# The query product on 64-by-64 parts of TensorE's array, in two passes between scores and values

## The chip, the cores and the metric

The kernel runs on one core of one Trainium2 chip. The metric is the device time of one execution in microseconds; the time of a kernel is the median of its runs. Before the change it is 2009.44 us, the median of three runs from 2009.4 to 2009.89 us. A second number is the span of one profiled execution, from its first to its last recorded instruction, which all rows of the profile refer to.

## The reference

One transformer layer in float32 on x of shape (32, 512, 256): a windowed attention with 16 query heads and 4 key/value heads, then a feed-forward product with a gated sum of eight low-rank terms.

```python
x = x + attn(_layernorm(x), wq, wk, wv, wo, q_norm_w, k_norm_w)
x = x + ffn(_layernorm(x), weight, gate_w, lora_U, lora_V)

def attn(x, ...):                      # DIM, H, KV, HD, WIN = 256, 16, 4, 64, 128
    q = rmsnorm((x @ wq.T).reshape(B, T, H, HD), q_norm_w)
    k = rmsnorm((x @ wk.T).reshape(B, T, KV, HD), k_norm_w)
    v = (x @ wv.T).reshape(B, T, KV, HD)
    k, v = jnp.repeat(k, 4, axis=2), jnp.repeat(v, 4, axis=2)
    scores = jnp.einsum('bqhd,bkhd->bhqk', q, k) / jnp.sqrt(HD)
    mask = (i >= j) & (i - j < WIN)
    a = jax.nn.softmax(jnp.where(mask, scores, -jnp.inf), axis=-1)
    return jnp.einsum('bhqk,bkhd->bqhd', a, v).reshape(B, T, H * HD) @ wo.T

def ffn(x, ...):                       # E, R = 8, 16
    gate = jax.nn.softmax(x @ gate_w.T)
    t = jnp.einsum('nh,erh->ner', x, lora_U)
    return x @ weight.T + jnp.einsum('ne,eor,ner->no', gate, lora_V, t) / R
```

## The kernel before

The 32 sequences of 512 tokens are cut into 128 tiles of 128 tokens, so four tiles make a sequence; tile t = 0 of a sequence has no tile before it. All tiles go through the same steps, and the kernel is a software pipeline over them: the function `slot(i)` (L805) lists one period, in which each step works on a tile that is some number of tiles behind i. The order in which every engine gets its instructions is written out by hand: `slot` for the middle, and two tables, FIRST and LAST, for the tiles at either end. There is no scheduler behind it; each engine's instructions stand in the order of these calls, and an engine whose next instruction has to wait holds back all that stands behind it.

The steps on TensorE, per tile, with the lines of the profile:

- `q_pe(gp)` (L418): the query product, in two halves of 512 columns (eight heads each), called with gp = 1 and gp = 0 at two places of a period. The stationary operand is xT, the transposed tile (two chunks of 128 features by 128 tokens), the moving one wq_sb. Each half is two matmuls on the full 128-by-128 array into one bank of PSUM, q0 or q1.
- `kv_pe` (L403): keys and values in one product of the same size.
- `s_pe(j)` (L535): scores of block j of 32 queries, j = 3, 2, 1, 0, eight matmuls on 64-by-64 parts of the array with up to 160 columns; four of them fill the array, two row halves by two column halves.
- `y_pe` and `yb_pe` (both L624): values, again on 64-by-64 parts with 256 columns. In `y_pe` the upper row half writes bank y0 and the lower one y1; in `yb_pe` rows and banks are exchanged. Between them stands `y_mark` (L653), a copy of one column of y1 on ScalarE (ACT) which `yb_pe` waits for, so that the two row halves never write one bank at one time. Tiles with t = 0 have no mixed part (`vd` and `other`) in `y_pe`.
- `o_pe` (L673), the output projection on the full array; `ug_pe` and `base_pe` (L720) and `lora_pe` (L775), the feed-forward products, full array, banks g and f.

In float32 the trace counts two records on TensorE for each matmul that is called.

ACT empties the banks: `q_copy` (L426) and `qsq` (L431) read each q bank, `kv_copy` and `ksq` (L409, L413) the kv bank, `y_copy` (L667) the y banks; `exps` (L562) reads the scores after DVE (VectorE) has merged the window's edges and taken the maxima (`s_merge` L546, `nmaxs` L551). POOL (GpSimd) raises the variances to the power -1/2 (`rsqrt`, L329), scales q and k (`qn` L463, `kn` L454) and the probabilities (`prob` L574), and masks (`pick` L605). DVE transposes by 32-by-32 blocks into a buffer of pieces; `move(n)` (L363) sends them in 16 DMAs on SP's queue to their places, from where ACT (kT, hT, uT) and TensorE (scores and values) read them.

PSUM has four single banks, B0 to B3, and two double ones, S0 and S1, for the scores. The table BANK says which products take turns in which bank in the middle of the kernel, and PLACES the exceptions of the tiles at the ends. A product waits until the last reader of the bank's former product is done.

In the middle of the kernel the order on TensorE was o(i-10), lora(i-16), q1(i-2), s2 and s3(i-5), y(i-8), q0(i-2), kv(i-2), yb(i-8), s1 and s0(i-5), g(i-12), f(i-15).

Of the kernel before, what the change touches and what calls it, by code (L numbers as in the profile page):

```python
# [8 lines left out]
F32 = mybir.dt.float32  # L9
# [5 lines left out]
P = 128  # L15
# [4 lines left out]
ND = D // P  # L20
# [10 lines left out]
def tile_window_attn_lora_ffn(  # L31
# [45 lines left out]
    nc = tc.nc  # L77
    B, T, _ = x.shape
    NT = T // P
    N = B * NT  # L80
    GP = KV // 2
# [29 lines left out]
    for tag, products in {  # L111
        "B0": "tk uT q1 kv",
        "B1": "ckv cqa cqb y0 o",
        "B2": "cf tq0 tq1 f y1",
        "B3": "hT q0 g",
        "S0": "s2 s0",
        "S1": "s3 s1",
    }.items():
        BANK.update(dict.fromkeys(products.split(), tag))
# [3 lines left out]
        ("ckv", 0): "B3",  # L123
        ("cqb", 0): "B2",
        ("kv", 0): "B3",
        ("cqa", 0): "B0",
        ("q1", 0): "B1",
        ("q0", 0): "B0",
        ("q1", 1): "B3",
        ("q0", 1): "B1",  # L130
        ("tk", 0): "B1",
        ("kv", 2): "B2",
        ("tq1", 0): "B3",
        ("q0", 2): "B1",
        ("tq0", 1): "B1",
        ("tq1", 1): "B3",
        ("tk", 1): "B3",
        ("q0", 3): "B2",
        ("kv", 3): "B2",
        ("tq0", 2): "B3",  # L140
        ("tq1", 2): "B3",
        ("q0", 4): "B1",
        ("q1", 4): "B2",
        ("kv", 4): "B3",
        ("q1", 5): "B2",
        ("q1", 6): "B3",
        ("y0", 0): "B2",
        ("y1", 0): "B1",
        ("q0", 6): "B0",
        ("kv", 6): "B1",  # L150
        ("y0", 2): "B2",
        ("y1", 2): "B1",
        ("o", 2): "B3",
        ("y0", 4): "B3",
        ("y1", 4): "B1",
        ("g", 0): "B2",
        ("o", 4): "B2",
        ("o", 5): "B2",
        ("g", 3): "B2",
        ("f", 0): "B1",  # L160
        ("o", 6): "B3",
        ("q0", -2): "B1",
        ("y0", -8): "B3",
        ("y1", -8): "B0",
        ("kv", -2): "B2",
        ("q0", -1): "B1",
        ("y0", -7): "B0",
        ("kv", -1): "B1",
        ("o", -8): "B2",
        ("y0", -6): "B3",  # L170
        ("y1", -6): "B0",
        ("y1", -5): "B0",
        ("o", -6): "B2",
        ("g", -8): "B0",
        ("y0", -4): "B3",
        ("y1", -4): "B0",
        ("o", -4): "B2",
        ("uT", -7): "B3",
        ("y1", -3): "B0",
        ("hT", -4): "B1",  # L180
        ("o", -3): "B0",
        ("y1", -2): "B3",
        ("o", -2): "B0",
        ("g", -6): "B0",
        ("f", -8): "B1",
        ("g", -5): "B2",
        ("uT", -6): "B2",
        ("y0", -1): "B3",
        ("y1", -1): "B0",
        ("g", -4): "B2",  # L190
        ("uT", -5): "B1",
        ("hT", -3): "B1",
        ("g", -3): "B1",
        ("uT", -4): "B1",
        ("o", -1): "B0",
        ("hT", -1): "B1",
        ("f", -5): "B1",
        ("g", -1): "B0",
        ("uT", -2): "B3",
        ("f", -4): "B3",  # L200
        ("f", -2): "B3",
# [166 lines left out]
    class Tile:  # L368
# [45 lines left out]

        def q_pe(self, gp):
            ps = self.bank(f"q{gp}")
            for c in range(ND):
                nc.tensor.matmul(  # L418
                    ps, self.xT[:, c, :], wq_sb[:, c, gp * 512 : (gp + 1) * 512],
                    start=(c == 0), stop=(c == ND - 1),  # L420
                )

# [228 lines left out]
        def y_mark(self):  # L651
            mark = small.tile([P, 1], F32, tag="mark", name=f"mark_{self.n}")
            nc.scalar.copy(mark, self.ps["y1"][:, :1])  # L653
# [151 lines left out]
    def slot(i):  # L805
        at(i - 4).trk()
        at(i - 6).exps(0)
        at(i - 12).hT_copy()
        at(i - 10).o_pe()
        at(i - 13).ln2_rs()  # L810
        at(i - 16).lora_pe()
        move(i - 7)
        at(i - 13).gmax()
        at(i - 16).store()
        at(i - 16).put()
        at(i - 2).q_pe(1)
        at(i - 5).kT_copy()
        at(i - 6).exps(1)
        at(i - 8).pick(1)
        at(i - 6).tr(2)  # L820
        at(i - 13).gexp()
        at(i - 10).o_add()
        at(i - 13).gmul()
        at(i - 2).qsq(1)
        at(i - 3).q_eps()
        at(i - 5).s_pe(2)
        at(i - 6).prob_den(0)
        at(i - 2).q_copy(1)
        at(i - 8).pick(0)
        at(i - 5).s_pe(3)  # L830
        at(i).ln1_stats()
        at(i - 8).y_pe()
        at(i - 5).s_merge(3)
        at(i - 5).nmaxs(3)
        at(i - 2).q_pe(0)
        at(i - 15).uT_copy()
        at(i - 5).s_merge(2)
        at(i - 2).kv_pe()
        at(i - 8).y_mark()
        at(i - 5).exps(3)  # L840
        at(i - 10).trh()
        at(i - 8).yb_pe()
        at(i - 2).q_copy(0)
        at(i - 1).trx()
        at(i - 6).prob(0)
        at(i - 5).nmaxs(2)
        at(i - 5).s_pe(1)
        at(i - 5).exps(2)
        at(i - 11).ln2_stats()
        at(i - 2).qsq(0)  # L850
        at(i - 5).s_pe(0)
        at(i - 1).ln1_rs()
        at(i - 3).pow()
        at(i - 3).kn()
        at(i - 6).vdiff()
        at(i - 6).tr(1)
        at(i - 13).tru()
        at(i - 3).qn()
        at(i - 6).tr(0)
        at(i - 12).ln2_eps()  # L860
        at(i - 6).tr(3)
        at(i - 8).y_copy(1)
        at(i - 5).s_merge(1)
        at(i - 5).prob_den(1)
        at(i - 12).ug_pe()
        at(i - 8).y_copy(0)
        at(i).ln1_eps()
        at(i - 5).nmaxs(1)
        at(i - 2).kv_copy()
        at(i - 2).ksq()  # L870
        at(i - 5).s_merge(0)
        at(i - 5).prob(1)
        at(i - 5).nmaxs(0)
        at(i - 3).trq()
        at(i - 2).ksum()
        at(i - 15).base_pe()
        at(i - 2).qsum()
        load_x(i + 1)
        load_blocks(i + 3)
# [3 lines left out]
        ldb:0 ldb:1 ldx:0 ldb:2 mean_kv:0 ldb:3 sub_kv:0 mean_qb:0 ln1_stats:0 trx:0 sub_qb:0 ldx:2  # L883
        mean_qa:0 ln1_eps:0 ldb:5 sub_qa:0 kv_pe:0 q_pe.1:0 q_pe.0:0 ln1_rs:0 ldx:1 kv_copy:0 ksq:0
        ln1_stats:2 trx:1 q_copy.1:0 qsq.1:0 ln1_stats:1 q_pe.0:1 ldx:5 ldx:4 ln1_eps:2 ln1_rs:2
        ldwv:0 ksum:0 ln1_stats:4 ln1_eps:1 qsq.0:0 ln1_rs:1 ldx:6 ln1_eps:4 ln1_rs:4 trx:3 qsum:0
        q_copy.0:0 q_eps:0 kv_pe:1 trx:2 ldx:8 kv_copy:1 q_pe.1:1 qsq.0:1 qsq.1:1 ksq:1 ksum:1 ldx:3
        q_copy.0:1 kv_pe:2 pow:0 q_pe.1:2 q_copy.1:1 qsum:1 kv_copy:2 q_eps:1 ksq:2 kn:0 tk_pe:0
        qn:0 tq_pe.1:0 ldx:9 kT_copy:0 ldb:4 tq_pe.0:0 ldb:6 ldx:7 qsq.1:2 ln1_stats:7 ldx:11 pow:1
        tq_copy.1:0 ksum:2 q_pe.0:2 tq_copy.0:0 ln1_stats:6 ln1_stats:3 s_pe.3:0 qsq.0:2 q_copy.0:2  # L890
        s_pe.2:0 ln1_eps:3 s_merge.3:0 nmaxs.3:0 qsum:2 s_merge.2:0 q_copy.1:2 kn:1 nmaxs.2:0
        kv_pe:3 ln1_stats:5 tk_pe:1 qn:1 exps.3:0 q_eps:2 q_pe.1:3 ldb:7 kT_copy:1 ln1_rs:3 ldb:10
        vdiff:2 kv_copy:3 pow:2 s_pe.1:0 exps.2:0 ldx:10 s_merge.1:0 ksq:3 trx:4 tq_pe.1:1 kn:2
        nmaxs.1:0 tq_pe.0:1 ksum:3 s_pe.0:0 s_merge.0:0 nmaxs.0:0 ln1_stats:8 q_pe.0:3 qsq.1:3
        tq_copy.1:1 prob_den.1:0 kv_pe:4 tq_copy.0:1 exps.1:0 qsq.0:3 qn:2 vdiff:3 exps.0:0 s_pe.3:1
        q_pe.0:4 s_pe.2:1 ldx:12 qsum:3 prob_den.0:0 q_copy.1:3 ln1_stats:10 q_eps:3 q_copy.0:3
        prob.1:0 kv_copy:4 tk_pe:2 ksq:4 s_merge.3:1 nmaxs.3:1 trx:5 tr.3:0 s_merge.2:1 tr.2:0
        tq_pe.0:2 prob.0:0 nmaxs.2:1 q_pe.1:4 exps.3:1 tq_copy.0:2 tr.1:0 pow:3 ln1_eps:5 tr.0:0
        s_pe.1:1 s_merge.1:1 kT_copy:2 trx:6 kn:3 tq_pe.1:2 qn:3 ksum:4 exps.2:1 ln1_eps:6
        prob_den.1:1 qsq.0:4 qsq.1:4 ln1_rs:5 nmaxs.1:1 tq_copy.1:2 qsum:4 q_copy.1:4 trq:3 kv_pe:5  # L900
        exps.1:1 kv_copy:5 q_eps:4 trk:3 q_copy.0:4 ksq:5 s_pe.0:1 q_pe.0:5 s_pe.3:2 s_merge.0:1
        nmaxs.0:1 prob.1:1 s_merge.3:2 exps.0:1 nmaxs.3:2 vdiff:0 tr.2:1 ln1_eps:7 ksum:5 q_pe.1:5
        trx:7 pow:4 tr.3:1 qsq.1:5 prob_den.0:1 qsq.0:5 exps.3:2 ldwo:0 ldwf:0 s_pe.2:2 ldb:9
        q_copy.0:5 kv_pe:6 s_merge.2:2 q_copy.1:5 kn:4 qn:4 ldb:11 nmaxs.2:2 qsum:5 prob.0:1 q_eps:5
        s_pe.1:2 trk:4 ldb:8 s_merge.1:2 q_pe.1:6 trq:4 ln1_rs:6 exps.2:2 kv_copy:6 mean_f:0
        nmaxs.1:2 s_pe.0:2 tr.1:1 q_pe.0:6 q_copy.1:6 qsq.1:6 pow:5 tr.0:1 s_merge.0:2 ksq:6
        q_pe.0:7 trx:9 move:0 exps.1:2 nmaxs.0:2 kn:5 sub_f:0 qsq.0:6 ksum:6 pick.1:0 kT_copy:3
        prob_den.1:2 pick.0:0 qsum:6 move:1 exps.0:2 qn:5 trk:5 s_pe.3:3 q_eps:6 q_copy.0:6 ln1_rs:7
# [108 lines left out]
    with tc.manual_schedule(engines={mybir.EngineType.PE, mybir.EngineType.Activation, mybir.EngineType.DVE, mybir.EngineType.Pool, mybir.EngineType.SP}):  # L1017
        in_order(FIRST, 0)
        for i in range(14, N - 1 + 1):
            slot(i)  # L1020
# [49 lines left out]
```

## Time and profile before

| what | value |
|---|---|
| median of three runs | 2009.44 us |
| the profiled execution | 2008.81 us |
| its span | 2007.1 us |
| TensorE (PE) busy, records | 1993.7 us, 18749 |
| VectorE (DVE) busy | 1746.1 us |
| GpSimd (POOL) busy | 1664.4 us |
| ScalarE (ACT) busy | 1533.2 us |
| q product, L418 | 493.6 us, 1024 records of 128x512 |
| scores, L535 | 296.4 us, 8000 records in the largest group |
| values, L624 | 276.9 us in 4096 records, 101.9 us in 1536 more |
| piece moves, L363 | 16 DMAs a tile on SP's queue |

A row of the timeline gives the start of a run of like instructions in microseconds from the span's start, how long the run lasted until the last one's end, the engine, the line, the operation, what it writes and reads, on TensorE the rows and columns of the array in use and the size of the moving operand, and the number of records. Ends on TensorE are modelled and neighbours overlap, so the distance from start to start is the time that a run takes. Brackets give the idle time before and what ended it. A few records can be missing.

### The profile page before, as it was taken

To read this page: it belongs to the slowest core of one execution; us is meant where nothing else is said; L and a number is where in the kernel's file an instruction comes from. 1 tells how busy PE (TensorE), PEld (TensorE's weight loads), DVE (VectorE), ACT (ScalarE), POOL (GpSimd) and SP (SyncE) were. 2 spreads that over 40 slices of the span, in tenths; PEclk is the share of its full clock that TensorE was granted. 3 is DMA by queue.
4 is the path that set the end of the run, shared out by engine and by line. 5 is a ranking of instruction groups with operands and counts; after the bars stand their busy time and mean duration, and the time that the engine had idled before them with its cause. 6 is when DMAs were issued, how large, how long until landed. Compare 5 with 4: busy or idle time off the path is not lost.

```text
span 2007.1 us, 56918 instructions
## 1 busy us (share of the span) xinstructions
PE 1993.7 (99%) x18749; PEld 1327.5 (66%) x18749; DVE 1746.1 (87%) x4667; ACT 1533.2 (76%) x6279; POOL 1664.4 (83%) x1291
## 2 busy tenths in 40 slices
PE   8999999999999999999999999999999999999998
PEld 4566666666666666666666666666666666666676
DVE  6998888888888988898888889888888888888894
ACT  6887777777777777777777777777777777777773
POOL 6998889888888888898888988888888889888873
PEclk9999999999999999999999999999999999999999
DMA  5666666666666666666666666766667667667663
GB/s 129 138 152 152 149 153 151 150 148 154 155 149 149 149 156 149 149 151 151 152 153 149 156 143 149 160 149 146 156 146 158 146 150 157 147 146 157 139 152 87
DMA packets 273043, 297.60 MB, mean 148 GB/s; under 512 B 172272, under 2 KB 206704, under 8 KB 272752
## 3 DMA queue, kind: packets, MB, share of 16 engines
q1 hardware_dynamic: 272208, 292.40, 65.3%
q8 instruction: 152, 2.49, 0.6%
q10 hardware_dynamic: 544, 1.57, 0.2%
q14 instruction: 139, 1.14, 0.2%
HBM read 36.71 MB, written 16.78 MB: 27 GB/s over the span
## 4 chain that ended last, share of the span: by engine, by line
PE 95%; SPq 2%; DVE 1%; ACT 1%; DMA 1%; issue 0%; DVEq 0%; ACTq 0%
PE q_ps L418 22%; PE o_ps L673 21%; PE y_ps L624 16%; PE s_ps L535 13%; PE kv_ps L403 11%; PE f_ps L720 5%; PE g_ps L720 4%; PE f_ps L775 3%; SPq L363 2%; ACT ex L562 0%; DVE nmax L551 0%; DMA wkv_sb<-in_wkv_dram 0%; DMA pT<-tr 0%; PE ckv_ps_mean L312 0%; DVE ss L440 0%
## 5 line engine op out<-in xcount | busy, mean ns | idle before, releaser
L562 ACT ACTIVATE ex<-s_ps,nmax 128x128 f32<-128x128 f32 x2048 | 724.8, 372 | 108.6 <-DVE nmax L551 98.1
L574 POOL TENSOR_TENSOR ex<-ex,rden 128x1024 f32<-128x1024 f32 x256 | 485.3, 1897 | 260.6 <-DVE rden L570 243.0
L418 PE MATMUL q_ps<-wq_sb,xT 128*128 128x512 f32 x1024 | 493.6, 605 | 0.0
L673 PE MATMUL o_ps<-wo_sb,yT 128*128 128x256 f32 x2048 | 463.5, 379 | 0.1
L329 POOL TENSOR_TENSOR rs<-ss_eps,minus_half 128x20 f32<-128x20 f32 x128 | 452.9, 3538 | 1.2 <-ACT ss_eps L446 1.1
L562 ACT ACTIVATION_READ_ACCUMULATOR ex<-s_ps,nmax 128x1 f32 x2048 | 431.4, 211 | 0.0
L673 PEld LDWEIGHTS o_ps<-wo_sb,yT 128*128 128x128 f32 x2048 | 388.3, 190 | 54.5 <-issue 1.6
L551 DVE TENSOR_REDUCE nmax<-s_ps 128x4 f32<-128x512 f32 x512 | 348.6, 681 | 9.0
L535 PEld LDWEIGHTS s_ps<-kT,pT 64*64 64x64 f32 x8000 | 246.6, 133 | 112.9 <-issue 56.0
L605 POOL TENSOR_SCALAR_AFFINE_SELECT other<-pT 64x512 f32<-64x512 f32 x384 | 289.9, 755 | 32.8 <-DMA pT<-tr 7.3
L418 PEld LDWEIGHTS q_ps<-wq_sb,xT 128*128 128x128 f32 x1024 | 183.8, 189 | 178.6 <-issue 137.0
L535 PE MATMUL s_ps<-kT,pT 64*64 64x160 f32 (+4 forms) x8000 | 296.4, 284 | 0.6 <-ACT ex L562 0.5
L624 PE MATMUL y_ps<-pT,kv 64*64 64x256 f32 x4096 | 276.9, 383 | 1.4 <-ACT mark L653 1.2
L431 ACT ACTIVATE qsq<-q_ps,ln_rs_a 128x512 f32<-128x512 f32 x256 | 178.6, 698 | 121.0 <-PE q_ps L418 118.6
L546 DVE COPY_PREDICATED s_ps<-over,s_ps 128x128 f32<-128x128 int32 x512 | 148.6, 290 | 112.8 <-ACT yT L667 78.0
L463 POOL TENSOR_TENSOR q<-q,rs 128x1024 f32<-128x1024 f32 x128 | 243.5, 1902 | 0.1
L585 DVE STREAM_TRANSPOSE tr<-ex 128x128 f32<-128x128 f32 (+3 forms) x512 | 239.4, 486 | 4.0 <-issue 1.0
L403 PE MATMUL kv_ps<-wkv_sb,xT 128*128 128x512 f32 x512 | 241.5, 594 | 0.0
L624 PEld LDWEIGHTS y_ps<-pT,kv 64*64 64x64 f32 x4096 | 145.2, 132 | 125.5 <-issue 88.9
L426 ACT ACTIVATE q<-q_ps,ln_rs_a 128x512 f32<-128x512 f32 x256 | 175.3, 686 | 33.5 <-PE q_ps L418 33.5
L403 PEld LDWEIGHTS kv_ps<-wkv_sb,xT 128*128 128x128 f32 x512 | 96.3, 190 | 120.3 <-issue 117.7
L440 DVE TENSOR_REDUCE ss<-qsq 128x16 f32<-128x1024 f32 x128 | 154.4, 1206 | 1.7 <-ACT qsq L431 1.6
(89 smaller groups left out, 2648.0 us busy)
## 6 DMA issues: line engine op xcount, KB each, us to landing
pT<-tr SPq DMA_DIRECT2D x1888, 116.0 KB, 2.3
xb<-in_x_dram SPq DMA_DIRECT2D x256, 64.0 KB, 2.4
x<-in_x_dram SPq DMA_DIRECT2D x128, 128.0 KB, 2.6
out_dram<-res SPq DMA_DIRECT2D x128, 128.0 KB, 1.8
pT<-tr SPq DMA_DIRECT2D x64, 104.0 KB, 2.2
pT<-tr SPq DMA_DIRECT2D x48, 112.0 KB, 2.3
pT<-tr SPq DMA_DIRECT2D x48, 76.0 KB, 2.1
wq_sb<-in_wq_dram ACTq DMA_DIRECT2D x1, 1024.0 KB
```

The costliest lines, as they stand in the source:

```text
L329: nc.gpsimd.tensor_tensor(o, v, minus_half[:, : o.shape[-1]], ALU.pow)
L403: nc.tensor.matmul(ps, self.xT[:, c, :], wkv_sb[:, c, :], start=(c == 0), stop=(c == ND - 1))
L418: nc.tensor.matmul(ps, self.xT[:, c, :], wq_sb[:, c, gp * 512 : (gp + 1) * 512], start=(c == 0), stop=(c == ND - 1),)
L463: nc.gpsimd.tensor_tensor(self.q_n.rearrange("p (g d) -> p g d", d=HD), self.q.rearrange("p g (h d) -> p (g h) d", d=HD), self.rs[:, :NH]. ...
L535: nc.tensor.matmul(ps[m * H : (m + 1) * H, half, gp, o0:n], qT[rows, gp * P + m * H : gp * P + (m + 1) * H], self.s.kT[rows, gp, k0 + o0 : ...
L551: nc.vector.tensor_reduce(self.nmax[j], ps[:, :, :, :P], AX.X, ALU.max, negate=True)
L562: nc.scalar.activation(self.ex[e][:, c, gp, half], ps[:, gp, half, :P], AF.Exp, bias=self.nmax[j][:, gp, half : half + 1], accum_out=self. ...
L574: nc.gpsimd.tensor_tensor(ex, ex, self.rden[e].rearrange("p c g a -> p (c g a)").unsqueeze(2).to_broadcast([P, 8, P]), ALU.mult,)
L585: nc.vector.transpose(to[:, :, :, j:], ex[:, :, :, : NB - j])
L605: nc.gpsimd.affine_select(out=self.other[gp][rows].rearrange("p h (c a q) -> p h c a q", c=2, a=2), in_=fr.rearrange("p h (c a q) -> p h c ...
L624: return nc.tensor.matmul(self.ps[f"y{e}"][half * HD : (half + 1) * HD, gp * 4 * H : (gp + 1) * 4 * H], v[:, v0 : v0 + HD], w.rearrange("p ...
L673: nc.tensor.matmul(ps[:, :D], self.yT[:, c].rearrange("p e t -> p (e t)"), wo_sb[:, c, :], start=(c == 0), stop=(c == NCH - 1),)
```

## The change

For 122 of the 128 tiles the query product is done on 64-by-64 parts, in two passes (`qa_pe`, `qb_pe`), with both banks q0 and q1 taken at the start of the first. In the first pass the upper row half (64 of a chunk's 128 features) computes into q0 and the lower into q1; in the second, rows and banks are exchanged, and the sums are complete. `q_mark`, a copy of one column of q1 on ACT, stands between them, as `y_mark` does for the values. Tiles 0 to 5 keep `q_pe`.

```diff
+        def q_product(self, r, start, stop):
+            for c in range(ND):
+                for m in range(2):
+                    for gp in (r, 1 - r):
+                        rows = slice((gp ^ r) * H, (gp ^ r) * H + H)
+                        nc.tensor.matmul(
+                            self.ps[f"q{gp}"][m * H : (m + 1) * H, :],
+                            self.xT[rows, c, m * H : (m + 1) * H],
+                            wq_sb[rows, c, gp * 512 : (gp + 1) * 512],
+                            start=(start and c == 0), stop=(stop and c == ND - 1),
+                            skip_group_check=True,
+                        )
+
+        def qa_pe(self):
+            for gp in range(GP):
+                self.bank(f"q{gp}")
+            self.q_product(0, True, False)
+
+        def qb_pe(self):
+            self.q_product(1, False, True)
+
+        def mark(self, what):
+            mark = small.tile([P, 1], F32, tag=f"mark_{what}", name=f"mark_{what}_{self.n}")
+            nc.scalar.copy(mark, self.ps[what][:, :1])
+
+        def q_mark(self):
+            self.mark("q1")
         def y_mark(self):
-            mark = small.tile([P, 1], F32, tag="mark", name=f"mark_{self.n}")
-            nc.scalar.copy(mark, self.ps["y1"][:, :1])
+            self.mark("y1")
```

The banks are shared out anew:

```diff
-        "B0": "tk uT q1 kv",
-        "B1": "ckv cqa cqb y0 o",
-        "B2": "cf tq0 tq1 f y1",
-        "B3": "hT q0 g",
+        "B0": "cf cqa tq0 q0 f",
+        "B1": "cqb tq1 q1 o",
+        "B2": "hT tk uT y0 g",
+        "B3": "ckv y1 kv",
```

The order of `slot`, of FIRST, of LAST and of PLACES is new throughout; `slot` runs from 17 on instead of 14. Its calls, by engine and in their order:

```python
# TensorE
s_pe(0) i-6; kv_pe i-3; ug_pe i-13; base_pe i-16; o_pe i-10; lora_pe i-16; s_pe(3) i-5; y_pe i-8;
s_pe(2) i-5; qa_pe i-2; yb_pe i-8; s_pe(1) i-5; qb_pe i-2
# ACT
ln2_eps i-12; y_copy(0) i-9; qsq(0), q_copy(1), q_copy(0), qsq(1), kv_copy, ksq i-3; kT_copy i-5;
gexp i-13; exps(1), exps(0) i-6; uT_copy i-15; hT_copy i-12; y_mark i-8; q_eps i-3; exps(3) i-5;
ln1_eps i-1; q_mark i-2; exps(2) i-5; y_copy(1) i-8
# DVE
s_merge(1) i-6; trh i-11; prob_den(1), vdiff i-6; tr(1) i-7; s_merge(0), nmaxs(1) i-6; tru i-14;
nmaxs(0) i-6; gmax i-13; trq i-4; ksum i-3; trk i-4; qsum i-3; gmul i-13; o_add i-10; store i-16;
trx i-2; s_merge(3) i-5; prob_den(0) i-6; nmaxs(3) i-5; tr(3) i-6; s_merge(2) i-5; ln2_stats i-11;
nmaxs(2) i-5; tr(2) i-6; ln1_stats i; tr(0) i-6
# POOL
qn i-4; ln1_rs i-2; pick(0), pick(1) i-8; prob(1), prob(0) i-6; pow, kn i-3; ln2_rs i-12
# SP
move(i-7); put i-16; load_x(i+1); load_blocks(i+3)
```

## The prediction

> **What bounds the kernel now.** I read the page first: the busy shares, the granted clock and the chain of waits.
>
> ```profile
> PE 1993.7 (99%) x18749; PEld 1327.5 (66%) x18749; DVE 1746.1 (87%) x4667; ACT 1533.2 (76%) x6279; POOL 1664.4 (83%) x1291
> PEclk9999999999999999999999999999999999999999
> PE 95%; SPq 2%; DVE 1%; ACT 1%; DMA 1%; issue 0%; DVEq 0%; ACTq 0%
> ```
>
> TensorE is busy in every slice at full granted clock and carries 95% of the chain; the sum of its waits is small (in the view of waits for PE, 5.3 us before the first weights and 4.6 us in seven later waits). So time can only come out of the stream of matmuls itself. A matmul's end in the trace is modelled, so I read start to start, in the timeline of one tile period in mid kernel:
>
> ```profile
> 1002.42 0.59 PE L775 MATMUL f_ps<-wv_sb,uT 128*128 128x256 f32 x2
> 1002.86 1.88 PE L418 MATMUL q_ps<-wq_sb,xT 128*128 128x512 f32 x4
> 1004.66 1.32 PE L535 MATMUL s_ps<-kT,pT 64*64 64x160 f32 x32
> 1005.80 1.04 PE L624 MATMUL y_ps<-pT,kv 64*64 64x256 f32 x16
> 1006.66 1.04 PE L624 MATMUL y_ps<-other,vd 64*64 64x256 f32 x16
> 1007.64 1.98 PE L418 MATMUL q_ps<-wq_sb,xT 128*128 128x512 f32 x4
> 1009.46 1.88 PE L403 MATMUL kv_ps<-wkv_sb,xT 128*128 128x512 f32 x4
> 1011.27 1.09 PE L624 MATMUL y_ps<-pT,kv 64*64 64x256 f32 x16
> 1012.18 1.27 PE L535 MATMUL s_ps<-kT,pT 64*64 64x160 f32 x32
> 1013.38 0.73 PE L720 MATMUL g_ps<-wf_sb,hT 128*128 128x136 f32 x4
> 1013.95 1.03 PE L720 MATMUL f_ps<-wf_sb,hT 128*128 128x256 f32 x4
> 1014.81 3.62 PE L673 MATMUL o_ps<-wo_sb,yT 128*128 128x256 f32 x16
> ```
>
> From one q1 to the next (1002.86 to 1018.70) the period is 15.84 us. The column 128*128 or 64*64 is the part of the array in use: it changes four times in a period, twice each way. The reader is to see that rows beside a change are longer than the same rows away from it. The clean price of a 512-column product comes from the start of the kernel, where products of one form follow each other:
>
> ```profile
> 15.02 5.31 PE L418 MATMUL q_ps<-wq_sb,xT 128*128 128x512 f32 x12
> 20.17 1.88 PE L403 MATMUL kv_ps<-wkv_sb,xT 128*128 128x512 f32 x4
> 21.89 1.88 PE L418 MATMUL q_ps<-wq_sb,xT 128*128 128x512 f32 x4
> ```
>
> Three products in 20.17 - 15.02 = 5.15 us: 1.72 us each.
>
> **The price of a change of form.** Full to quarter: kv before y takes 1011.27 - 1009.46 = 1.81, so 0.09 over 1.72; the y group just after it takes 0.91 against 0.86 away from a change, 0.05 more. Quarter to full: the last y group before q0 takes 0.98 against 0.86, 0.12 more; that q0 takes 1.82 against 1.72, 0.10 more. A round trip costs 0.09 + 0.05 + 0.12 + 0.10 = 0.36 us. Quarter to quarter costs nothing visible: s after q1 takes 1.14 and s after y 1012.18 to 1013.38 = 1.20, whose 0.06 and more is explained by the change at its end; the two y groups follow each other at 0.86.
>
> **The change, part by part.** (a) Round trips removed. I counted changes of form in the built order of TensorE's instructions: 542 before, 314 after. Steady periods go from four to two, since everything on quarters (s3, y, s2, first q pass, yb, s1, second q pass, s0) now stands together, and kv, g, f, o, lora together. 228 changes are 114 round trips: 114 x 0.36 = -41.0 us.
>
> (b) The q product itself. 122 of 128 tiles use quarters (six early ones keep the old form): 16 calls of 64x64x512 per tile for 4 of 128x128x512; the trace counts two records for each. Four calls run together on the four quarters, so a pass is 4 such fours of 512 columns. No row shows 512 columns on quarters. Nearest is y, with the same pattern (row halves into two banks, column halves into the two halves of a bank): 16 records of 256 columns are four fours in 0.86 us, 0.216 each; o on the full array has 16 records of 256 columns in 1018.26 - 1014.81 = 3.45, 0.216 each. Quarter fours and full instructions of one length cost the same, so a pass is 1.72, as before: 0. From below: s runs 160 columns in (1.14 - 0.05) / 8 = 0.136, 0.85 ns a column against 0.84 for y; longer rows could save 0.01 ns x 512 x 8 x 122 = -5 us at most. From above: if each four lost the 0.05 that the first one after a change loses, 8 x 0.05 x 122 = +49 us. I take 0, by y's row.
>
> There is a rule against this change. The Trainium skill, "TensorEngine Tiling (Array Packing)", section Performance Considerations, puts some 60 cycles of overhead on each matmul; read as a cost per instruction at the 2.4 GHz in the opening table of "TensorE: Matmul & The Clock Gate", that is 25 ns for 24 more records a tile, an estimate of 24 x 0.025 x 122 = +73 us, and the kernel would be slower. The trace disagrees already: y's 16 records at 25 ns each of overhead would add 0.4 us to a group that takes 0.86, and quarters are as dense there as the full array.
>
> (c) One more ACT instruction per tile, q_mark, on 122 tiles. The y mark is 159 ns long and the next instruction starts 0.06 us after it: 7 us over the run on an engine idle 24% of the time. The second pass waits for it, which must not show: between the passes stand yb and s1, 0.86 + 0.54 = 1.40 us. Behind the mark on ACT stand exps2, y_copy1, y_copy0, then the four q reads.
>
> (d) The order. Instruction counts on DVE and POOL stay the same, SP has one fewer. What can go wrong is a wait. I laid out the new period by hand, t = 0 at s0: s0 to 0.54; kv 0.66 to 2.48; g 2.94; f 3.80; o 7.25; lora 7.69; s3 7.78 to 8.38; y 10.10; s2 10.65; first q pass 12.37; yb 13.23; s1 13.78; second pass 15.50. Against it ACT, start to start:
>
> ```profile
> 1002.95 0.37 ACT L562 ACTIVATE ex<-s_ps,nmax 128x128 f32<-128x128 f32 x1
> 1004.32 0.33 ACT L740 ACTIVATE g<-lg,gmax 128x8 f32<-128x8 f32 x1
> 1007.77 0.16 ACT L653 COPY mark<-y_ps 128x1 f32<-128x1 f32 x1 [1.38 <-PE y_ps L624]
> ```
>
> Four exps take 1004.32 - 1002.95 = 1.37; each q read 0.58, kv_copy 0.57, ksq 0.4, kT_copy 0.42, a y_copy 0.48, small ones 0.1. I allow 0.2 us from a matmul's end to its reader. y_mark at 10.3, exps3 to 11.9, q_mark waits for the first pass until 12.7 (needed by the second pass at 13.78: 1.1 spare), exps2 to 14.0 (s0's bank at 15.50: 1.5 spare), both y_copies to 15.1. q reads from 15.7: q0's bank free at 17.7 = 2.2 in the next period, f needs it at 2.94: 0.7 spare; q1's bank free at 2.8, o needs it at 3.80: 1.0 spare. Then kv_copy, ksq, kT, gate exp, exps1 to 5.8 (s3 at 7.78: 2.0 spare), exps0 to 7.2 (s2 at 10.10), then idle until y_mark. So the burst of four q reads, which is new, is hidden by s0, kv and g; without that cover the whole 2.3 us would stand before f. DVE: h's add waits for o at 7.5, store for lora at 7.9, xT transpose to 8.6 (first pass at 10.65: 2.0 spare), nmax3 by 9.7 (exps3 10.5: 0.8), nmax2 by 12.3 (exps2 12.7: 0.4, the tightest, but 0.6 us of waiting for the second pass lies behind it on ACT). POOL has 1664.4 / 128 = 13.0 us of work a period, 14 with pick in it; its probability product waits for prob_den0 some 1.3 us, which is its spare. SP: 16 piece moves take 11 us and the rest 2.7, of 15.5; the moves are issued at 5.3 and land by 3.0 of the next period, where kT_copy takes them at 3.7. No wait reaches TensorE: 0.
>
> (e) First 17 and last 16 periods are new orders that rows do not price. All of TensorE's idle time is 13.4 us before; 5.3 of it is the first load and 3.2 the tail after the last matmul (2007.1 - 2003.9), so 4.9 is stalls. Bounds: -5 (all gone) to +10 (threefold). I take +1.6, since the middle gained speed but loads and first softmaxes did not.
>
> Sum: span 2007.1 - 41.0 = 1966.1; the profiled execution lies 1.7 above its span (2008.81): 1967.8; the median of the runs, 2009.44, is 0.6 above that: 1968.4; with 1.6 for the ends **1970.0 us**.
>
> **Rivals.** *A queue takes back a part.* The spare is thin (0.4 to 1.1 us) and DVE rises to 1746 / 1970 = 89%, POOL to 85%. For it: four q reads in a row on ACT, the y mark's wait of 1.38 us shows how much of ACT's time hangs on TensorE, and DVE runs beside POOL with drifting durations. Against: every spare is positive and ACT still idles about 2.5 us before y_mark. A shortfall of 0.15 us in each of 111 steady periods gives 1970 + 17 = 1987; 0.35 us would eat the gain.
>
> *Quarters cost more at 512 columns* (the slower one). Place: each four of the q passes; price 0.05 us, the loss seen where the next weights were not yet in; 976 fours: 1970 + 49 = 2019. It decides from 0.040 us a four. For it: four weight loads where one was, all reading xT, and two quarters stream the same wq rows. Against: s does just that with kT and runs dense at 160 columns, where a load has a third of the time to hide.
>
> *The change does not do what it says*: TensorE drains between passes anyway, since both write the same banks. Then the 114 round trips stay partly: half of them gives 1990. Against: y does the same between own and mixed terms, and yb followed by s showed no gap. I count it with the first rival.
>
> **How the numbers follow.** Forecast 0.76, own range 1961 to 1979 (ends -5 to +10). First rival 0.17, mostly 1979 to 2000. Second 0.07. The range reaches into the first rival: 1960 to 1995, leaving out its tail and the second. Telling no change takes about 0.2%, 4 us: faster 0.76 + 0.13 = 0.89, same 0.03, slower 0.01 + 0.07 = 0.08.
>
> **What would show it.** Right: two changes of form in each steady period, the period 15.5 us where y has its mixed part, q on quarters 1.7 us a pass, f's first row with no idle before it. The first rival: PE waits for ACT q or qsq before f or o, for nmax or exps before s, or for q_mark. The second: q passes of 1.9 us with PE unbroken. Wrong altogether: PE busy below 97%.

## The result and the profile after

The changed kernel takes 2003.3 us in the median of seven runs (2002.39 to 2005.05) against 2009.53 us for the kernel before in seven: a ratio of 0.9968, interval 0.9957 to 0.998. It is faster by 0.3%, where the forecast had 2%. Its profiled span is 2003.2 us.

From the page of the changed kernel, busy time and share of each engine, the granted clock in 40 slices, and the shares of the chain that ended last:

```profile
PE 1988.5 (99%) x21677; PEld 1527.8 (76%) x21677; DVE 1762.9 (88%) x4667; ACT 1523.6 (76%) x6401; POOL 1684.5 (84%) x1291
...
PEclk9999999999999999999999999999999999999999
...
PE 86%; SPq 5%; POOL 3%; DVE 3%; DMA 1%; ACT 1%; issue 1%; DVEq 0%; POOLq 0%; ACTq 0%
```

TensorE is still busy in 99% of the span at full clock. The records on it grew by 2928, which is 24 more for each of 122 tiles, as the change says. PE's share of the chain fell from 95% to 86%; the rest went to engines that feed it, but that is no time lost by itself: the view of waits for TensorE, in us in total, times and longest, begins like this:

```profile
PE ckv_ps_mean L323 <- DMA wkv_sb<-in_wkv_dram: 5.1, 1, 5.1
PE s_ps L578 <- ACT ex L605: 3.1, 7, 1.0
PE y_ps L667 <- PE s_ps L578: 0.8, 1, 0.8
```

After the first weights some 5.6 us of waits are left in the list, 4.6 before. So the missing 33 us stand in no wait that this view shows. They are found in the timeline of TensorE, one period in mid kernel:

```profile
1009.81 0.96 PE L578 MATMUL s_ps<-kT,pT 64*64 64x160 f32 x16
...
1017.30 0.59 PE L817 MATMUL f_ps<-wv_sb,uT 128*128 128x256 f32 x2
1017.82 0.77 PE L578 MATMUL s_ps<-kT,pT 64*64 64x160 f32 x16
1018.42 1.24 PE L667 MATMUL y_ps<-pT,kv 64*64 64x256 f32 x14
1019.28 0.38 PE L667 MATMUL y_ps<-other,vd 64*64 64x256 f32 x1
1019.32 0.38 PE L667 MATMUL y_ps<-pT,kv 64*64 64x256 f32 x2
1019.50 1.02 PE L667 MATMUL y_ps<-other,vd 64*64 64x256 f32 x13
...
1025.53 0.96 PE L578 MATMUL s_ps<-kT,pT 64*64 64x160 f32 x16
1026.42 1.98 PE L414 MATMUL kv_ps<-wkv_sb,xT 128*128 128x512 f32 x4
1028.24 0.63 PE L762 MATMUL g_ps<-wf_sb,hT 128*128 128x136 f32 x4
1028.70 1.03 PE L762 MATMUL f_ps<-wf_sb,hT 128*128 128x256 f32 x4
1029.57 3.62 PE L715 MATMUL o_ps<-wo_sb,yT 128*128 128x256 f32 x16
```

The form changes twice in the period, as planned. The row to look at is y, which is broken into 14, 1, 2 and 13 records: one group's first records start before the last ones of the group ahead. The four quarters of the array are out of step. In the records, y's first quarter starts at 1018.418 and the three others at 1018.612 to 1018.626, some 0.2 us behind. They stay apart through the whole stretch until kv, which needs the full array and waits for the last quarter. The last block of scores takes 0.89 us up to kv (1025.53 to 1026.42), where the forecast had 0.66, and s0 to s0 is 1025.53 - 1009.81 = 15.72 us instead of the 15.50 laid out.

A semaphore record on TensorE's queue stands for one or two waits that an instruction carries. The view of the line of the values counts them (number, shortest, median and longest in ns), first in the kernel before, then in the changed one:

```profile
L624 PEldq EVENT_SEMAPHORE  x535: 51/51/3946, 67.6 to 1985.4; - x179
```

```profile
L667 PEldq EVENT_SEMAPHORE  x873: 51/51/1045, 65.7 to 1980.4; - x175
```

There are 338 more, three a tile. In the built order of a steady tile, y's first two matmuls carry nine waits before and 14 after; in the trace the nine stand in four semaphore records and the 14 in seven, and two of each on weight loads. The reason is the block s2: it reads the same moved pieces as y, stood ahead of it before and took the waits on two of the DMA queues off its hands; the change moves it behind y. And only one block of scores (s3, 0.54 us) now stands ahead of y where two stood (1.09 us). In the period shown, the semaphore records ahead of y follow each other at 1017.846, 1017.957, 1018.062, 1018.168, 1018.294, 1018.400 and 1018.506, about 0.106 us apart, and y's second weight load follows at 1018.582.

From here on a *quarter stretch* is the time from s3's first matmul to kv's first, and a *full stretch* from kv's first to s3's first, both start to start, in the 105 or so steady periods between 250 and 1850 us. Quarter stretches are of three kinds: in one period of four y has no mixed part; in another the scores are *short* (those of a tile with t = 0, where s3 has 128 columns instead of 160); in the other two y has its mixed part and the scores are full. In the changed kernel the 52 quarter stretches with the mixed part and full scores take 8.63 us in the mean (8.60 in the median), the 27 with the mixed part and short scores 7.77 (7.73), the 26 without the mixed part 7.75 (7.73); the full stretch is 7.13.

### The profile page after: what moved, and what is told of

Its sections match the earlier page's. It is cut to its first block, busy times and chain, and to the rows that moved or that the text cites. A ratio compares the mean times of both kernels' runs of the same rounds, so it can differ in the third digit from the quotient of the medians.

```text
span 2003.2 us, 63108 instructions
## 1 busy us (share of the span) xinstructions
PE 1988.5 (99%) x21677; PEld 1527.8 (76%) x21677; DVE 1762.9 (88%) x4667; ACT 1523.6 (76%) x6401; POOL 1684.5 (84%) x1291
## 4 chain that ended last, share of the span: by engine, by line
PE 86%; SPq 5%; POOL 3%; DVE 3%; DMA 1%; ACT 1%; issue 1%; DVEq 0%; POOLq 0%; ACTq 0%
PE o_ps L715 19%; PE q_ps L442 18%; PE y_ps L667 14%; PE s_ps L578 12%; PE kv_ps L414 11%; SPq L374 5%; PE f_ps L762 5%; PE g_ps L762 3%; PE f_ps L817 2%; POOL rs L340 1%; DMA pT<-tr 1%; POOL ex L617 1%; PE q_ps L430 1%; ACT ex L605 1%; POOL q L506 0%
## 5 line engine op out<-in xcount | busy, mean ns | idle before, releaser
L442 PE MATMUL q_ps<-wq_sb,xT 64*64 64x512 f32 x3904 | 522.8, 590 | 0.0
L605 ACT ACTIVATION_READ_ACCUMULATOR ex<-s_ps,nmax 128x1 f32 x2048 | 444.2, 217 | 0.0
L578 PE MATMUL s_ps<-kT,pT 64*64 64x160 f32 (+4 forms) x8000 | 425.3, 284 | 3.3 <-ACT ex L605 2.7
L578 PEld LDWEIGHTS s_ps<-kT,pT 64*64 64x64 f32 x8000 | 360.2, 133 | 83.5 <-issue 17.3
L667 PE MATMUL y_ps<-pT,kv 64*64 64x256 f32 x4096 | 331.7, 380 | 1.2 <-PE s_ps L578 0.8
L442 PEld LDWEIGHTS q_ps<-wq_sb,xT 64*64 64x64 f32 x3904 | 260.0, 133 | 71.7 <-issue 23.5
L667 PEld LDWEIGHTS y_ps<-pT,kv 64*64 64x64 f32 x4096 | 225.5, 133 | 59.2 <-issue 10.5
L628 DVE STREAM_TRANSPOSE tr<-ex 128x128 f32<-128x128 f32 (+3 forms) x512 | 252.2, 494 | 4.4 <-DMA pT<-tr 1.5
L461 ACT COPY mark_y<-y_ps 128x1 f32<-128x1 f32 x128 | 20.6, 161 | 265.8 <-PE y_ps L667 265.7
L521 DVE STREAM_TRANSPOSE tr<-q 128x1024 f32<-128x1024 f32 x125 | 154.2, 1233 | 2.1 <-POOL q L506 2.1
```

The lines of the kernel that those rows point to most:

```text
L442: nc.tensor.matmul(self.ps[f"q{gp}"][m * H : (m + 1) * H, :], self.xT[rows, c, m * H : (m + 1) * H], wq_sb[rows, c, gp * 512 : (gp + 1) * ...
L578: nc.tensor.matmul(ps[m * H : (m + 1) * H, half, gp, o0:n], qT[rows, gp * P + m * H : gp * P + (m + 1) * H], self.s.kT[rows, gp, k0 + o0 : ...
L605: nc.scalar.activation(self.ex[e][:, c, gp, half], ps[:, gp, half, :P], AF.Exp, bias=self.nmax[j][:, gp, half : half + 1], accum_out=self. ...
L628: nc.vector.transpose(to[:, :, :, j:], ex[:, :, :, : NB - j])
L667: return nc.tensor.matmul(self.ps[f"y{e}"][half * HD : (half + 1) * HD, gp * 4 * H : (gp + 1) * 4 * H], v[:, v0 : v0 + HD], w.rearrange("p ...
```

## The experiments

**Theory A**: TensorE's queue works off the waits of an instruction one after the other, some 0.1 us each, though they are fulfilled (the run with one column touched shows that this is the price of a record and not of a wait); with 14 of them on y and one block of scores in front, the queue falls behind the array. **Theory B**: the pieces themselves land late. **Rival C**: banks or ACT hold the scores back. A fourth reading is the forecast's own: quarter passes cost more, or a round trip less, than priced.

### s2 put back ahead of y

```diff
         at(i - 8).pick(1)
+        at(i - 5).s_pe(2)
         at(i - 8).y_pe()
-        at(i - 5).s_pe(2)
```

> The changed kernel with one edit: in the steady period s_pe(2) stands ahead of y_pe again, so that y's waits for the piece moves (14 in the built order, 9 when s2 has taken its own share) are worked off by TensorE's queue under 1.09 us of scores and not under 0.54 us. Theory A (TensorE's queue takes some 0.1 us for each of these waits, and in the changed kernel the last of them end after s3 has run out): the quarter stretch of a period falls from 8.60 to 8.36 us with a mixed y part, from 7.73 to 7.50 without, from 7.73 to about 7.35 where s has few columns; the average loss of 0.29 us a period, times 111, goes: 2003.3 - 31 = 1972 us (1968 to 1978). Rival B (64-by-64 parts of q are dearer than they looked, or the four quarters running out of step is what costs): no change, 2001 to 2005. Rival C (s2 ahead now waits for its bank, since exps0 is late): back to 2000 or more, with TensorE waiting for ACT before s2.

Measured: 1987.78 us, ratio 0.9894 (0.9877 to 0.991). Four fifths of 1% come back from exchanging two lines, but 16 us less than A alone gives. Quarter stretches without the mixed part fall to 7.50 us in the mean; those with it and full scores to 8.44 (8.36 in the median, which the next experiment shows as the floor); those with short scores stay at 7.82 in the mean (7.63 in the median), where the floor is 7.39. The semaphore records of y fall from 873 to 651, to five a tile, for ten waits where the expectation had nine. In exchange s2 now asks for its bank sooner. The wait of its weight load, in the changed kernel and then here:

```profile
PEld s_ps L578 <- ACT ex L605: 18.2, 43, 1.2
```

```profile
PEld s_ps L578 <- ACT ex L605: 28.1, 67, 1.2
```

There are 24 more such waits. Added up over the 106 quarter stretches, the time above the floors is these 16 us. Nineteen of these are over 0.3 us too long and hold 11.4 us; in eleven of them the trace shows a weight load of the scores waiting for exps (ACT ex), which is C's wait, though C was not tried by itself. Of the other 4.6 us, 3.0 stand in stretches with short scores: there y is broken as before, and none of the 27 comes within 0.19 us of the floor. So A holds for most of it, and the cure by order has its own price.

### One small matmul ahead of lora that takes the waits

```diff
+        def touch(self):
+            nc.tensor.matmul(
+                self.ps["f"][:, D : D + NB], mean_m, moved[self.i + 8][:, :, PO],
+                start=False, stop=False, skip_group_check=True,
+            )
...
         at(i - 10).o_pe()
+        at(i - 16).touch()
         at(i - 16).lora_pe()
```

It reads one column of each moved piece, so it waits for all moves of the tile, behind the 3.45 us of o; it writes four columns of bank f that nothing reads. This holds for the later kernels with such a matmul too.

> The changed kernel, order kept (s3, y, s2), with one small matmul more per steady period, between o and lora: 4 columns that read one column of each of the moved pieces, into columns of bank f that nothing reads. It takes all the waits for the 16 moves upon itself, so that y waits for none, and they are worked off under o's 3.45 us. Theory A: the loss of 0.29 us a period goes, the small matmul costs 0.06 to 0.2 us: 2003.3 - 111 x (0.29 - 0.13) = 1985 us (1978 to 1994); y follows s3 without a gap. Rival B (the place of y right behind one score block, or quarters out of step, whatever the waits): y still comes late on three quarters, and the time rises by the small matmul, 2010 to 2025 us.

Measured: 1994.41 us, ratio 0.9927 (0.9912 to 0.9941), 0.4 us above A's band and far from B's. From the timeline of TensorE:

```profile
1012.88 0.28 PE L817 MATMUL f_ps<-pT,mean_m 128*128 128x4 f32 x2
1013.02 0.68 PE L823 MATMUL f_ps<-wv_sb,uT 128*128 128x256 f32 x2
1013.62 0.77 PE L578 MATMUL s_ps<-kT,pT 64*64 64x160 f32 x16
1014.22 1.04 PE L667 MATMUL y_ps<-pT,kv 64*64 64x256 f32 x16
1015.08 1.04 PE L667 MATMUL y_ps<-other,vd 64*64 64x256 f32 x16
1015.95 0.72 PE L578 MATMUL s_ps<-kT,pT 64*64 64x160 f32 x16
```

y is whole again, 16 and 16 records of 0.86 us, and the quarters keep step. All quarter stretches of a kind now agree within 0.01 us: 8.36 us with the mixed part, 7.39 with short scores and 7.49 without the mixed part. These are the floors; the changed kernel's means lie 0.28, 0.38 and 0.26 above them. The full stretch pays: 7.35 us instead of 7.13, of which 0.14 stands between the touch and lora and 0.07 in lora's row. At 0.22 us in each of 111 periods the touch costs 24 us, and 1994.4 - 24 = 1970, close to the forecast. The semaphore records of y and of the touch:

```profile
L667 PEldq EVENT_SEMAPHORE  x207: 51/51/1244, 66.3 to 1971.9; - x104
...
L817 PEldq EVENT_SEMAPHORE  x444: 51/51/1255, 184.3 to 1863.3; - x148
```

### The q passes on the full array, in the same places

```diff
+        def q_full(self, gp):
+            for c in range(ND):
+                nc.tensor.matmul(
+                    self.ps[f"q{gp}"], self.xT[:, c, :], wq_sb[:, c, gp * 512 : (gp + 1) * 512],
+                    start=(c == 0), stop=(c == ND - 1),
+                )
...
-            self.q_product(0, True, False)
+            self.q_full(1)
...
-            self.q_product(1, False, True)
+            self.q_full(0)
```

> The changed kernel with q on the full array again, in the same places and banks: gp 1 where the first pass stood, gp 0 where the second stood. Two round trips of form come back in each of 111 steady periods and some at the ends. If a round trip costs 0.36 us and a quarter pass costs the same as half of the full product: 2003.3 + 111 x 0.72 + about 5 = 2088 us (2078 to 2096). Rival B (quarter passes are dearer by 0.03 to 0.05 us a four, which would have eaten the gain): 4 fours twice a period, 0.24 to 0.4 us, come off again: 2045 to 2062.

Measured: 2084.51 us, ratio to the kernel before 1.0372 (1.0357 to 1.0388), 81.2 us above the changed kernel. Its trace has 780 changes of form, 466 more than the changed kernel's 314, so 233 round trips: 81.2 / 233 = 0.349 us for one. The timeline shows where they sit:

```profile
1011.30 1.98 PE L452 MATMUL q_ps<-wq_sb,xT 128*128 128x512 f32 x4
1013.21 1.09 PE L674 MATMUL y_ps<-pT,kv 64*64 64x256 f32 x16
1014.12 0.72 PE L585 MATMUL s_ps<-kT,pT 64*64 64x160 f32 x16
1014.78 1.98 PE L452 MATMUL q_ps<-wq_sb,xT 128*128 128x512 f32 x4
1016.69 0.78 PE L585 MATMUL s_ps<-kT,pT 64*64 64x160 f32 x16
```

A full pass with a change on both sides takes 1.91 us (1011.30 to 1013.21); a row of scores ahead of one takes 0.66 instead of 0.54. A quarter pass therefore costs what a full one costs away from a change, and the round trip is priced right.

### The kernel before, with s2 behind y

```diff
-        at(i - 5).s_pe(2)
         at(i - 6).prob_den(0)
...
         at(i - 8).y_pe()
+        at(i - 5).s_pe(2)
         at(i - 5).s_merge(3)
```

The q product stays on the full array. If the loss needs no quarter pass of q, it must appear here.

> The kernel before with one edit: s_pe(2) behind y_pe in the steady period, as in the changed kernel; q stays on the full array. Theory A: the loss comes without any q on quarters: y follows a single score block and all its waits, 0.24 to 0.44 us in each of 114 periods: 2009.5 + 33 = 2042 us (2032 to 2048). Rival B (the loss comes with q on quarters): 2008 to 2012.

Measured: 2053.71 us, ratio 1.022 (1.0205 to 1.0235), 44 us slower than the kernel before and more than expected. The timeline has the same break, though here the q pass behind s2 is a full one:

```profile
1012.74 0.67 PE L535 MATMUL s_ps<-kT,pT 64*64 64x128 f32 x16
1013.22 1.10 PE L624 MATMUL y_ps<-pT,kv 64*64 64x256 f32 x13
1014.09 0.38 PE L624 MATMUL y_ps<-other,vd 64*64 64x256 f32 x1
1014.12 0.42 PE L624 MATMUL y_ps<-pT,kv 64*64 64x256 f32 x3
1014.30 0.88 PE L624 MATMUL y_ps<-other,vd 64*64 64x256 f32 x12
```

So the loss belongs to the place of s2 and not to the new q product. Its size is not A's alone: in the mean, stretches of s2, s3 and y with the mixed part are 0.45 us longer than before with full scores and 0.23 with short ones, and 26 of the 101 stretches of g, f, o, lora and q lengthen, by up to 0.57 us. TensorE's waits for exps grow from 3 times, 0.7 us in all, to 29 times, 6.7 us, which is C's kind of wait. Why the loss is larger than in the changed kernel, though y has six records a tile here and not seven, is open.

### An empty instruction that waits for the moves

```diff
+    def arrived(n):
+        nop = nc.tensor.nop("arrived")
+        for ins in moves[n]:
+            tc.add_manual_dep(nop.ins, ins.ins.name, ...)
...
         at(i - 10).o_pe()
+        arrived(i - 8)
         at(i - 16).lora_pe()
```

It stands where the touch stood and waits for the same moves, but y keeps its own waits in the built order. When y comes up, every piece has long landed.

> The changed kernel, order kept, with an instruction on TensorE's queue between o and lora that computes nothing and waits until all 16 piece moves have landed. The built order shows that y's own waits stay where they are; they are only certain to be fulfilled by then. Theory A (each wait costs its time in the queue, fulfilled or not): the loss between s3 and y stays, 0.24 us in a period with full s and 0.44 in one with short s, and the time stays at 2003 us (2000 to 2007). Rival A2 (the moves land late, and y waits for them): the lateness moves before lora or vanishes, y follows s3 at once, and the time either falls to 1975 or shows idle time of TensorE before lora.

Measured: 2003.98 us, ratio 0.997 (0.9959 to 0.9982), as the changed kernel. The quarter stretch with the mixed part and full scores is 8.63 us in the mean, again the same, and y keeps its 873 semaphore records. The empty instruction's own waits, four records a tile behind o, leave the full stretch at 7.13 us. Waits that are already fulfilled cost as much as before, so B falls: the pieces are not late, the waits themselves take the time.

### The touch read as bfloat16

Shown against the touch in float32:

```diff
+            bf = mybir.dt.bfloat16
             nc.tensor.matmul(
-                self.ps["f"][:, D : D + NB], mean_m, moved[self.i + 8][:, :, PO],
+                self.ps["f"][:, D : D + NB], mean_m.bitcast(bf)[:, :P],
+                moved[self.i + 8].bitcast(bf)[:, :, 2 * PO + 1],
```

> As the kernel with the small matmul (1994.4 us), but the small matmul reads the same bytes as bf16, so that the profile should show one record for it and not two. There it took 0.21 us a period: 0.14 from its first record to lora's and 0.07 more in lora. One record should take about half: 1994.4 - 111 x 0.10 = 1983 us (1978 to 1991), and the quarter stretch stays at 8.36, 7.49 and 7.39 us. If the small matmul costs the same with one record: 1994.

Measured: 1983.28 us, ratio 0.9868 (0.9852 to 0.9885); the fastest kernel of this study, 20 us below the changed one. In the timeline the touch is one record, lora follows 0.03 us after it, and every step on quarters has its clean length:

```profile
1006.17 0.17 PE L818 MATMUL f_ps<-pT,mean_m 128*128 128x4 bf16 x1
1006.20 0.68 PE L825 MATMUL f_ps<-wv_sb,uT 128*128 128x256 f32 x2
1006.80 0.78 PE L578 MATMUL s_ps<-kT,pT 64*64 64x160 f32 x16
1007.40 1.04 PE L667 MATMUL y_ps<-pT,kv 64*64 64x256 f32 x16
1008.26 1.04 PE L667 MATMUL y_ps<-other,vd 64*64 64x256 f32 x16
1009.12 0.72 PE L578 MATMUL s_ps<-kT,pT 64*64 64x160 f32 x16
1009.67 1.90 PE L442 MATMUL q_ps<-wq_sb,xT 64*64 64x512 f32 x16
1011.38 1.04 PE L667 MATMUL y_ps<-pT,kv 64*64 64x256 f32 x16
```

The quarter stretches are at their floors again, 8.36, 7.39 and 7.49 us, the full stretch is 7.24. Against the changed kernel that is 52 x 0.28 + 27 x 0.38 + 26 x 0.26 = 31 us gained and 106 x 0.11 = 12 us paid, 19 net; measured 20.

### Only one of the four columns touched

Shown against the bfloat16 touch with four columns:

```diff
-                self.ps["f"][:, D : D + NB], mean_m.bitcast(bf)[:, :P],
-                moved[self.i + 8].bitcast(bf)[:, :, 2 * PO + 1],
+                self.ps["f"][:, D : D + 1], mean_m.bitcast(bf)[:, :P],
+                moved[self.i + 8].bitcast(bf)[:, :1, 2 * PO + 1],
```

> The small bf16 matmul between o and lora now reads only one of the four columns of pieces, so in the built order it takes four of the DMA waits and leaves y's first two matmuls ten waits instead of 14. Theory A, waits are worked off one after the other about 0.106 us apart and only what the cover in front does not hide costs: four fewer are 0.42 us, more than the 0.235 us lost in a period with a full s3, so the stretch on quarters comes back to its floor (8.36 us with the mixed y) there; where s3 is short the loss of 0.44 us falls to about 0.02. Time as with all four columns touched, 1983 to 1986 us. If the loss came from one particular late move or from the form of y itself and not from the number of waits, it would stay where that move is among the ten: about 0.2 us a period, 2003 + 12 = 2015 us with the price of the small matmul.

Measured: 1991.47 us, ratio 0.991 (0.9894 to 0.9927): between the two numbers. The semaphore records of y tell why:

```profile
L667 PEldq EVENT_SEMAPHORE  x651: 51/51/1149, 65.7 to 1966.4; - x163
```

That is 222 fewer than in the changed kernel, two a tile for the four waits taken away, since a record holds up to two. So 0.106 us is the price of a record, and my expectation had priced four records where two go. Two are 0.21 us, and by 0.21 us the median stretch falls in each of the three kinds: from 8.60 to 8.39, from 7.73 to 7.52 with short scores and from 7.73 to 7.52 without the mixed part. Against the floors 0.03, 0.13 and 0.03 us are left. It also fits that the loss in the changed kernel is 0.11 us larger with short scores (0.35 against 0.24 in the median), where the cover, s3, is 0.11 us shorter: the last of y's quarters starts 0.80 us after s3 in both. A stands, counted in records. The means lie a little higher (8.41, 7.54 and 7.53 us); in some periods s3 also waits for ACT.

### The touch in the kernel before

The same bfloat16 touch with four columns, between o and lora of the kernel before.

> The kernel before with the same small bf16 matmul (four columns) between o and lora, result unused. Theory A: before, two blocks of scores stand in front of y, its nine waits are covered, and the touch has nothing to give back; it costs 0.106 us in each of some 111 periods and saves what is above the floor in y's group, 0.014 us a period: 2009.5 + 11.8 - 1.5 = 2020 us, between 2017 and 2022. Rival, the touch speeds up something else (weights ready earlier, the form of the array): a gain as in the changed kernel, 2009.5 - 20 = 1990 us.

Measured: 2022.72 us, ratio 1.0063 (1.0048 to 1.0078), 0.7 us above the expected band. The stretch of g, f, o, lora and q grows from 7.13 to 7.24 us; that of s2, s3 and y stays at 2.97 us in the median with full scores and comes down from 2.68 to 2.65 in the mean with short ones. Where y's waits are covered, the touch only costs. It is not a gain by itself, so what it gave the changed kernel was the waits.

### The touch with one column of weights

Shown against the bfloat16 touch with four columns:

```diff
-                self.ps["f"][:, D : D + NB], mean_m.bitcast(bf)[:, :P],
+                self.ps["f"][:1, D : D + NB], mean_m.bitcast(bf)[:, :1],
```

> The changed kernel with the small bf16 matmul made narrow: one column of weights instead of 128 (one row of the bank written, result unused). It asks where the 0.106 us of the small matmul comes from. If from the weight load of 128 columns (its record lasts 0.098 us), most of it goes and the time falls by up to 111 x 0.08 = 9 us, to 1974 to 1977 us. If from the change between float32 and bf16 or a fixed price of one matmul, it stays at 1983 us.

Measured: 2003.05 us, ratio 0.9967 (0.9955 to 0.9979); neither of the two. The timeline:

```profile
1013.31 3.62 PE L715 MATMUL o_ps<-wo_sb,yT 128*128 128x256 f32 x16
1016.86 0.17 PE L818 MATMUL f_ps<-pT,mean_m 128*1 128x4 bf16 x1
1016.96 0.70 PE L825 MATMUL f_ps<-wv_sb,uT 128*128 128x256 f32 x2
1017.59 0.64 PE L578 MATMUL s_ps<-kT,pT 64*64 64x160 f32 x12
```

The array is now used as 128*1, another form. o takes 3.55 us up to the touch instead of 3.46, the touch 0.10 instead of 0.03, and the full stretch is 7.42 us instead of 7.24. So the narrow touch costs 0.18 us a period more than the wide one and eats the gain. Two more changes of form would account for it, but no run separates them from the narrow shape itself, and where the 0.11 us of the wide touch come from stays open.

### The first q pass ahead of y

A try at covering y's waits with work that must be done anyway: `qa_pe` goes between s3 and y, with the steps on DVE and ACT reordered to suit.

```diff
+        at(i - 2).trx()
         at(i - 13).gmul()
...
-        at(i - 2).trx()
         at(i - 12).hT_copy()
         at(i - 8).pick(1)
+        at(i - 2).qa_pe()
         at(i - 8).y_pe()
         at(i - 5).s_pe(2)
+        at(i - 2).q_mark()
+        at(i - 3).q_eps()
         at(i - 6).prob(1)
-        at(i - 8).y_mark()
...
         at(i - 5).nmaxs(3)
+        at(i - 5).exps(3)
+        at(i - 8).y_mark()
+        at(i - 8).yb_pe()
         at(i - 3).kn()
-        at(i - 2).qa_pe()
-        at(i - 8).yb_pe()
-        at(i - 5).exps(3)
...
```

> The changed kernel with the first pass of q moved between s3 and y (order s3, first pass, y, s2, yb, s1, second pass, s0); xT's transpose comes ahead of the gate product and h's add on DVE, and on ACT q_mark, q_eps and exps3 come ahead of y_mark. y's waits then have the 1.72 us of the first pass as cover, and nothing is added. Theory A: the loss of 0.29 us a period goes: 2003.3 - 31 = 1972 us (1968 to 1980) if no new wait appears. Rival (the first pass now waits for DVE, whose store of res must free q0's bank: lora ends at 7.7 us of the period, the pass would start at 8.4): up to 0.3 us a period, 1980 to 2000, with TensorE waiting before the first pass.

Measured: 2167.99 us, ratio 1.0787 (1.0771 to 1.0803): a clear miss, far above both numbers. On TensorE the q pass waits for its bank:

```profile
1014.34 1.95 PE L442 MATMUL q_ps<-wq_sb,xT 64*64 64x512 f32 x16 [0.57 <-DVE res L824]
1016.11 1.04 PE L667 MATMUL y_ps<-pT,kv 64*64 64x256 f32 x16
1016.98 1.04 PE L667 MATMUL y_ps<-other,vd 64*64 64x256 f32 x16
```

and on DVE, in the same period:

```profile
1018.63 0.29 DVE L589 COPY_PREDICATED s_ps<-over,s_ps 128x128 f32<-128x128 int32 x1 [2.74 <-PE s_ps L578]
```

y keeps step here, whole rows of 0.87 and 0.86 us. But s2 comes 1.7 us later, DVE stands 2.74 us before it, and behind that instruction wait the maxima of s2 and, in the next period, the addition `res` whose bank the q pass needs. As I read these rows, two engines wait for each other in a circle, and the circle sets the period; no run takes the circle apart.

## Why the prediction was off, by its own steps

**(a) Round trips, -41.0 us: right.** Taking each row at its own column rate, a clean quarter stretch is 0.158 us longer than its rows and a full one 0.195, together 0.353 us for a round trip against 0.36 predicted. The full q passes give 0.349. The Trainium skill says in "TensorEngine Tiling (Array Packing)", section Tiling Modes, that a change of the tiling mode drains TensorE; the runs agree and give it this size; the narrow touch fits it for a third form.

**(b) The q product, 0: right.** Its passes take 1.71 and 1.72 us in the clean period above (1009.67 to 1011.38 is the first), the price of a full one. The overhead of some 60 cycles for each matmul (the Trainium skill, "TensorEngine Tiling (Array Packing)", section Performance Considerations), from which the prediction worked out an estimate of 73 us, does not show: had it come on top of each, the full passes would have been faster by it, and they only cost their round trips.

**(c) q_mark, hidden: right.** In the waits of the changed kernel it is the mark that waits for TensorE, not the reverse:

```profile
ACT mark_q L461 <- PE q_ps L442: 49.9, 110, 0.8
```

**(d) "No wait reaches TensorE: 0": wrong, and this is the step that failed.** I followed which bank is free when and which engine is done when, and those sums nearly held: before TensorE's matmuls the view of waits shows none for q_mark or for the q reads of the steady periods, and seven for exps, 3.1 us in all. What I left out is what a wait costs when it is already fulfilled. I noted that s2 moves behind y as an order of matmuls and did not ask which waits it had carried for y. y's first two matmuls went from nine to 14 waits, in the trace from four to seven semaphore records, and their cover from two blocks of scores to one. The price is 0.26 to 0.28 us a period in the mean with full scores and 0.38 with short ones, 31 us in all, and it goes when the touch carries the waits.

**(e) The ends, +1.6: too small.** With rows and changes of form taken out, and beside the wait for the first weights, the first 250 us hold some 14 us of other time against some 7.6 before, 6.4 more; the last 250 us hold 2 to 3 us more, about what (d) takes in the steady periods among them. Which instructions of the first tiles lose it was not looked into by experiment.

The sum, each term from the two traces with 0.179 us as the mean price of one change:

| term | predicted, us | measured, us |
|---|---|---|
| 228 changes of form fewer | -41.0 | -40.8 |
| steady periods, (d) | 0 | +30.5 |
| first 250 us, (e) | +1.6 with the last | +6.4 |
| span | -39.4 | -3.9 |

The rival "A queue takes back a part" had the size, 0.15 to 0.35 us a period, but for another reason: it looked for ACT, DVE or POOL to be late, and beyond the 3.1 us for exps none is. The queue was TensorE's own, so that this rival's size fits is luck. "Quarters cost more" and "TensorE drains between passes" are both excluded by the clean passes.

## What to carry to other kernels

When a step is moved in a hand-written order, count the waits of the instructions around it in the built order as well as the times at which data is ready: a step that came first may have carried waits for all that read the same data. Waits on a dense engine want work queued in front of them that lasts longer than they take to work off (here 0.106 us for each semaphore record), and one cheap instruction placed behind a long row can carry them for everyone. Look for it not in the view of waits but in rows that break into odd numbers of records.

## What the runs showed of the hardware

- Fulfilled waits are not free on TensorE's queue: semaphore records, of one or two waits each, follow each other 0.106 us apart in the median, and with all pieces landed ahead the time is the same (2003.98 against 2003.3 us).
- The four 64-by-64 quarters run on by themselves: a delay of 0.2 us in three of them stays through some 8 us of products and is paid once, at the next instruction on the full array.
- A 4-column matmul lengthens the full stretch by 0.22 us in float32 and by 0.11 in bfloat16, between two full products; with one column of weights, which the trace shows as another form of the array, by 0.29.
